# Moving edge loads, one head's row stores and the logit reads out of a prologue

## The chip, the cores and the metric

The kernel runs on one core of one Trainium2 chip. The metric is the device time of one execution in microseconds (us), as the median of several runs. Each profile shows one execution. Chips differ from one series of runs to the next: the median of the kernel before was 3262 to 3279 us in the five series of this study. So kernels are compared by their ratio to the kernel before in the same rounds. An execution can also fall in a slower state; all timed runs used here are of the fast one.

## The reference, cut to what matters

Two graph layers follow one another. Layer 0, the only one concerned, is attention over a given graph of 4096 nodes with four heads of 64 columns:

```python
h = relu(layernorm(x)) @ W            # (4096, 256), 4 heads
src, dst = h . a[:64], h . a[64:]     # logits per node and head
e = leaky_relu(src[:, :, None] + dst.T[None]);  e = where(adj > 0, e, -9e15)
x = x + layernorm(softmax(e) @ h)     # softmax and product per head
# layer 1: top-p attention with two steps over x, much longer, unchanged
```

The kernel never forms the softmax. For each source node it prepares rows of exponentials times `h`, splits them exactly into three bf16 parts, and multiplies them by 0/1 masks that say on which side of the leaky ReLU an edge falls.

## The kernel before

Layer 0 begins with a prologue over 32 blocks of 128 nodes; sixteen passes (four groups of 1024 targets by four heads) follow. One turn of the prologue, cut:

```python
for g in range(NB // 4):                      # NB = 32 blocks, in groups of four
    mv = rows.tile(..., name="mv4")           # 3 buffers
    ... moments of four blocks (VectorE), rs and nmr (GpSimd, 2 buffers each)
    for i in range(4):
        b = 4 * g + i
        nc.scalar.activation(hb, x4[:, i, :], AF.Relu, scale=rs, bias=nmr)
        ... 2 transposes of hb into pt
        nc.scalar.copy(hT, pt)
        ... 2 products of hT with wx into pm  (fp32, 264 columns)
        nc.vector.tensor_copy(sd_c[:, :, :, b], ...)             # logits
        ... uv = exp(logits) and rows times exp  (ScalarE, VectorE)
        parts = rows.tile([P, H, 2, W3 + 1], BF16, name="parts", bufs=6)
        set1 = nc.gpsimd.memset(parts[:, :, :, W3:], 1.0)
        nc.scalar.copy(parts[:, :, :, :W1], uv)                  # first part
        nc.vector.tensor_tensor(uv, uv, parts[...], ALU.subtract)
        if b % 3 == 2 and len(ax) < NB // 4:                     # 8 edge loads
            with tc.issue_after(set1.ins):
                ax.append(edges(0, len(ax)))                     # 1 MB each, from POOL
        ... second and third part
        nc.gpsimd.tensor_copy(ut0[b // QUARTER][:, b % QUARTER], parts[:, 0])
        nc.scalar.dma_start(uv_d[:, :, b]..., parts)             # row store, 4 heads
nc.sync.dma_start(s_d..., sT)                                    # logits to memory
```

The first pass starts with `g`, the mask input of targets: `g = relu(BIG * (src + dst))` from `sr`, the logits of 1024 targets spread over all partitions (read back from memory), then masks `m` against the edges `ax`, then products with the rows `ut`. Compute engines follow the written order in layer 0; the queue of SP (loads and stores of edges, rows and logits) does not and issues whatever is ready.

Of the kernel before, what the change touches and what calls it, by code (L numbers as in the profile page):

```python
# [11 lines left out]
F32 = mybir.dt.float32  # L12
F32R = mybir.dt.float32r
BF16 = mybir.dt.bfloat16
# [10 lines left out]
P = 128  # L25
# [12 lines left out]
G0 = 8  # L38
# [9 lines left out]
def gat_then_top_p_diffusion(  # L48
# [18 lines left out]
    nc = tc.nc  # L67
# [4 lines left out]
    NB = N // P  # L72
# [5 lines left out]
    small = ctx.enter_context(tc.tile_pool(name="small", bufs=4))  # L78
# [73 lines left out]
    with tc.tile_pool(name="l0", bufs=1) as l0, tc.tile_pool(name="l0a", bufs=9) as l0a, \  # L152
# [12 lines left out]
        ax = []  # L165
        QUARTER = NB // 4

        def quarter():
            return l0u.tile([P, QUARTER, 2, W3 + 1], BF16, name="ut")

        ut0 = [quarter() for q in range(4)]
        with tc.tile_pool(name="l0r", bufs=3) as rows, tc.tile_pool(name="l0w", bufs=1) as l0w, \
                tc.tile_pool(name="ps2", bufs=2, space=PSUM) as ps2:
            a_r = row_vector(a, "a_r", l0w)
            wx = l0w.tile([P, KC, D + 2 * H], F32, name="wx")
            nc.sync.dma_start(wx[:, :, :D], w.rearrange("(k p) m -> p k m", p=P))
            for k in range(KC):
                for i in range(2):
                    pr = l0w.tile([P, H, HD], F32, name="pr")
                    nc.vector.tensor_mul(pr, wx[:, k, :D].rearrange("p (h d) -> p h d", h=H),  # L180
                                         a_r[:, None, ts(i, HD)].to_broadcast([P, H, HD]))
                    nc.vector.reduce_sum(wx[:, k, ds(D + i * H, H)], pr, axis=AX.X)
            xs = [l0w.tile([P, 4, D], F32, name=f"x{g}") for g in range(NB // 4)]
            for g, x4 in enumerate(xs):
                nc.sync.dma_start(x4, x[ts(g, 4 * P), :].rearrange("(b p) d -> p b d", p=P))
            for g in range(NB // 4):
                x4 = xs[g]
                mv = rows.tile([P, 4, nc.vector.BN_AGGR_DIM], F32, name="mv4")
                for i in range(4):
                    moments_of(mv[:, i, :], x4[:, i, :])  # L190
                rs, nmr = steps(mv, 4, rows)
                for i in range(4):
                    b = 4 * g + i
                    hb = rows.tile([P, D], F32, name="hb")
                    nc.scalar.activation(hb, x4[:, i, :], AF.Relu, scale=rs[:, i:i + 1], bias=nmr[:, i:i + 1])
                    pt = ps2.tile([P, KC, P], F32, name="tp")
                    for k in range(KC):
                        nc.tensor.transpose(pt[:, k, :], hb[:, ts(k, P)], ident)
                    hT = rows.tile([P, KC, P], F32, name="hT")
                    nc.scalar.copy(hT, pt)  # L200
                    pm = ps2.tile([P, 512], F32, name="mm", bufs=3)
                    for k in range(KC):
                        nc.tensor.matmul(pm[:, :D + 2 * H], hT[:, k, :], wx[:, k, :], start=(k == 0), stop=(k == KC - 1))
                    nc.vector.tensor_copy(sd_c[:, :, :, b], pm[:, ds(D, 2 * H)].rearrange("p (t h) -> p t h", t=2))
                    uv = rows.tile([P, H, 2, W1], F32, name="uv")
                    for t, scale in enumerate((1.0, ALPHA)):
                        nc.scalar.activation(uv[:, :, t, HD:], pm[:, ds(D + H, H)][:, :, None], AF.Exp, scale=scale)
                    for t in range(2):
                        nc.vector.tensor_mul(uv[:, :, t, :HD], pm[:, :D].rearrange("p (h d) -> p h d", h=H),
                                             uv[:, :, t, HD:].to_broadcast([P, H, HD]))  # L210
                    parts = rows.tile([P, H, 2, W3 + 1], BF16, name="parts", bufs=6)
                    set1 = nc.gpsimd.memset(parts[:, :, :, W3:], 1.0)
                    nc.scalar.copy(parts[:, :, :, :W1], uv)
                    nc.vector.tensor_tensor(uv, uv, parts[:, :, :, :W1], ALU.subtract)
                    if b % 3 == 2 and len(ax) < NB // 4:
                        with tc.issue_after(set1.ins):
                            ax.append(edges(0, len(ax)))
                    nc.scalar.copy(parts[:, :, :, ds(W1, W1)], uv)
                    nc.vector.tensor_tensor(parts[:, :, :, ds(2 * W1, W1)], uv, parts[:, :, :, ds(W1, W1)], ALU.subtract)
                    nc.gpsimd.tensor_copy(ut0[b // QUARTER][:, b % QUARTER], parts[:, 0])  # L220
                    nc.scalar.dma_start(uv_d[:, :, b].rearrange("h p t w -> p h t w"), parts)
            pt = ps2.tile([P, KC, P], F32, name="tp")
            nc.tensor.transpose(pt[:, 0, :], s_c.rearrange("p h b -> p (h b)"), ident)
            sT = l0w.tile([P, P], F32, name="sT")
            nc.scalar.copy(sT, pt[:, 0, :])
            nc.sync.dma_start(s_d.rearrange("h (b i) -> (h b) i", b=NB), sT)
            w1_s, w2_s, w1_r = (l0w.tile(s, F32, name=x) for x, s in (
                ("w1_s", [P, KC, DA]), ("w2_s", [DA, DA]), ("w1_r", [DA, KC, P])))
            nc.scalar.dma_start(w1_s, w1_t.rearrange("(k p) m -> p k m", p=P))
            nc.scalar.dma_start(w2_s, w2_t)  # L230
            pt = ps2.tile([P, KC, P], F32, name="tp")
            for k in range(KC):
                nc.tensor.transpose(pt[:DA, k, :], w1_s[:, k, :], ident)
            nc.scalar.copy(w1_r, pt[:DA])
            for k in range(KC):
                pm = ps2.tile([P, 512], F32, name="mm", bufs=3)
                nc.tensor.matmul(pm[:, :DA], w1_r[:, k, :], w2_s, start=True, stop=True)
                nc.scalar.copy(wkq[:, k, DA:], pm[:, :DA])
            nc.vector.tensor_scalar(d_big, d_c, BIG, None, ALU.mult)

            for e, sign in zip(e_c, (1.0, -1.0)):
                nc.vector.tensor_scalar(e, s_c, sign * (1.0 - ALPHA), 0.0, ALU.mult, ALU.min)
                nc.scalar.activation(e, e, AF.Exp)

        with tc.tile_pool(name="l0m", bufs=3) as l0m, \
# [8 lines left out]
            def sources(k):  # L254

                ig, h = passes[k]
                sr = l0s.tile([P, G0 * P], F32, name="sr")
                nc.sync.dma_start(sr, s_d[h:h + 1, ts(ig, G0 * P)].to_broadcast([P, G0 * P]))
                shared[k] = SimpleNamespace(sr=sr, ut=[])

            def weighted(k, q):
                ut = quarter()
                nc.sync.dma_start(ut, uv_d[passes[k][1], :, ts(q, QUARTER)])
                shared[k].ut.append(ut)
# [10 lines left out]
            def masks(k, p, g):  # L275
                a = ax[p // 2][:, ds(2 * (p % 2), 2), :]
                m = [l0m.tile([P, 2, G0 * P], BF16, name=f"m{t}") for t in range(2)]
                nc.vector.tensor_tensor(m[0], g, a, ALU.min)  # L278
                nc.vector.tensor_tensor(m[1], a, m[0], ALU.subtract)  # L279
                return m  # L280

            def products(k, p, m):
# [75 lines left out]
            def sign_stage(n):  # L358
                if n < len(todo):
                    k, p = todo[n]  # L360
                    if n == 0:
                        sources(0)
                        shared[0].ut = ut0
                    gs[n] = signs(k, p)

            def mask_stage(n):
                if n < len(todo):
                    k, p = todo[n]
                    ig, h = passes[k]
                    if p % 4 == 0:  # L370

                        nq = k * 4 + p // 4 + 2
                        if 4 <= nq < 4 * len(passes):
                            if nq % 4 == 0:
                                sources(nq // 4)
                            weighted(nq // 4, nq % 4)
                    ms[n] = masks(k, p, gs.pop(n))
                    if h == 1 and p % 2:
                        nc.sync.dma_start(adj_d[ts(p // 2, 4), :, ts(ig, G0 * P)].rearrange("c p i -> p c i"), ax[p // 2])
                    if h == H - 1 and ig + 1 < NB // G0 and p % 2:  # L380
                        next_ax.append(edges(ig + 1, p // 2))
                    if h == H - 1 and p == PAIRS - 1:
                        ax[:] = next_ax
                        next_ax.clear()
# [724 lines left out]
```

## Time and profile before

| what | value |
|---|---|
| time | 3261.56 us, median of 3 (3259.44 to 3265.22); a fourth run came with the result |
| first row store issued | 31.46 us |
| last row store issued | 143.91 us, so 112.45 / 31 = 3.63 us a block |
| first `g` | 151.07 us |
| first pass closed (first `st<-acc` on ScalarE) | 199.16 us |
| layer 1's first big row operation (`big<-e,lowered`) | 1531.22 us |

### The profile page before, as it was taken

How to read it: one execution, taken by the hardware profiler on the slowest of the kernel's cores; microseconds unless marked ns; L12 is line 12 of the kernel's file. 1: busy time of each engine (PE TensorE's matmuls, PEld its weight loads, DVE VectorE, ACT ScalarE, POOL GpSimd, SP SyncE). 2: the span in 40 equal slices, each digit the busy share in tenths (PEclk: the TensorE clock that was granted, in tenths of full speed). 3: DMA queues.
4: the chain of work that ended last, by engine and by line, in shares of the span. 5: the costliest groups of instructions: out<-in, count | busy, mean ns of one | idle time of the engine just before them, and what ended most of it. 6: DMA issues, size and time to landing. Idle time of an engine off the chain costs nothing. (4 is left out here: it accounts for less than half of the span.)

```text
span 3276.4 us, 51761 instructions
## 1 busy us (share of the span) xinstructions
PE 2973.4 (91%) x19213; PEld 2417.6 (74%) x19213; DVE 2656.6 (81%) x5020; ACT 1952.7 (60%) x2903; POOL 1266.9 (39%) x1793
## 2 busy tenths in 40 slices
PE   4499899898989999986899999999879999999996
PEld 2299799797977888874677777777757777777785
DVE  6598899998976555546999999999469988888894
ACT  5588687786862110016577776775266777776742
POOL 3200100201000000003798998899015656656530
PEclk8699999999999999997899999999889999999998
DMA  9825639356225555520000000000100000000000
GB/s 260 228 83 144 204 113 255 117 142 206 73 85 181 165 177 164 161 89 1 10 19 15 16 20 15 15 18 17 62 13 10 25 20 25 22 22 25 20 27 13
DMA packets 198314, 268.48 MB, mean 82 GB/s; under 512 B 13728, under 2 KB 155552, under 8 KB 198048
## 3 DMA queue, kind: packets, MB, share of 16 engines
q1 hardware_dynamic: 152272, 207.99, 19.4%
q0 software_dynamic: 16896, 33.56, 5.7%
q10 hardware_dynamic: 28880, 23.48, 2.3%
q8 instruction: 155, 2.54, 0.3%
q14 instruction: 111, 0.91, 0.1%
HBM read 226.77 MB, written 71.76 MB: 91 GB/s over the span
## 5 line engine op out<-in xcount | busy, mean ns | idle before, releaser
L799 PE MATMUL acc<-X,eT 128*128 128x256 f32 x4160 | 978.4, 381 | 0.8 <-ACT eT L793 0.8
L799 PEld LDWEIGHTS acc<-X,eT 128*128 128x128 f32 x4160 | 762.6, 191 | 90.1 <-ACT eT L793 1.9
L291 PE MATMUL acc<-ut,m 128*128 128x195 bf16 (+1 forms) x8192 | 732.2, 249 | 82.3 <-DVE m L279 49.7
L291 PEld LDWEIGHTS <-m 128*128 128x128 bf16 x8192 | 703.4, 98 | 111.1 <-DVE m L279 66.9
L272 ACT ACTIVATE g<-sr,d_big 128x1024 bf16<-128x1024 f32 x512 | 550.6, 1178 | 50.2 <-DVE m L278 40.6
L618 ACT ACTIVATE void<-e,c 128x2048 int8<-128x2048 f32 x244 | 490.4, 2010 | 0.6
L611 ACT ACTIVATE e<-mm,nm 128x1024 f32<-128x1024 f32 x256 | 285.9, 1117 | 341.2 <-PE mm L488 338.1
L432 PE MATMUL racc<-hl,ar 128*128 128x512 f32 x2048 | 469.4, 391 | 16.8 <-issue 10.0
L432 PEld LDWEIGHTS racc<-hl,ar 128*128 128x128 f32 x2048 | 384.5, 188 | 101.5 <-issue 10.8
L791 PEld LDWEIGHTS tp<-ident,e 128*128 128x128 f32 x2080 | 246.8, 143 | 224.2 <-issue 126.6
L793 ACT COPY eT<-tp 128x512 f32<-128x512 f32 x520 | 303.4, 584 | 168.9 <-PE tp L791 168.1
L791 PE MATMUL tp<-ident,e 128*128 128x128 f32 x2080 | 327.9, 281 | 57.0 <-DVE e L728 42.8
L278 DVE TENSOR_TENSOR m<-g,ax 128x2048 bf16<-128x2048 bf16 x256 | 311.7, 1218 | 41.8 <-ACT g L272 38.8
L707 DVE MAX8 cand<-big 128x8 f32<-128x228 f32 (+1 forms) x1088 | 343.9, 395 | 0.1
L279 DVE TENSOR_TENSOR m<-ax,m 128x2048 bf16<-128x2048 bf16 x256 | 317.1, 1239 | 26.9 <-DVE m L278 1.4
L488 PE MATMUL mm<-kT,qT 64*128 64x512 f32 x1024 | 304.8, 678 | 33.5 <-ACT e L611 33.5
L428 DVE CAST ar<-at 128x1024 fp32r<-128x1024 bf16 x256 | 177.0, 692 | 169.8 <-PE racc L432 167.3
L694 DVE SCALAR_TENSOR_TENSOR big<-e,lowered 128x4096 f32<-128x4096 f32 x64 | 286.8, 4482 | 20.9 <-POOL lowered L639 20.9
L728 DVE SCALAR_TENSOR_TENSOR e<-e,found 128x4096 f32<-128x4096 f32 x64 | 286.7, 4480 | 0.0
L443 ACT ACTIVATE xf<-xf,rinv 128x256 f32<-128x256 f32 x64 | 32.7, 510 | 373.3 <-DVE xf L442 373.3
L648 POOL TENSOR_TENSOR sums<-sums 128x4 f32<-128x4 f32 (+1 forms) x64 | 106.4, 1662 | 378.8 <-ACT void L618 231.1
L488 PEld LDWEIGHTS mm<-kT,qT 64*128 64x128 f32 x1024 | 84.3, 196 | 130.6 <-issue 66.7
(245 smaller groups left out, 3269.4 us busy)
## 6 DMA issues: line engine op xcount, KB each, us to landing
at<-adj_d SPq DMA_DIRECT2D x256, 256.0 KB, 3.0
ut<-uv_d SPq DMA_DIRECT2D x60, 784.0 KB, 4.3
ax<-in_adj_t_dram POOLq DMA_DIRECT2D x32, 1024.0 KB, 13.6
adj_d<-ax SPq DMA_DIRECT2D x32, 1024.0 KB, 11.5
uv_d<-parts ACTq DMA_DIRECT2D x32, 392.0 KB, 8.2
xf<-xf_d SPq DMA_DIRECT2D x65, 128.0 KB, 2.0
sr<-s_d SPq DMA_DIRECT2D x16, 512.0 KB, 4.7
xf_d<-xf ACTq DMA_DIRECT2D x64, 128.0 KB, 2.4
```

The lines of the kernel that those rows point to most:

```text
L272: nc.scalar.activation(g[:, c, :], shared[k].sr, AF.Relu, scale=BIG, bias=d_big[:, h, j:j + 1])
L278: nc.vector.tensor_tensor(m[0], g, a, ALU.min)
L279: nc.vector.tensor_tensor(m[1], a, m[0], ALU.subtract)
L291: nc.tensor.matmul(shared[k].acc[i][:, t, :cols], m[t][:, c, ts(i, P)], shared[k].ut[j // QUARTER][:, j % QUARTER, t, :cols], start=(j == ...
L432: nc.tensor.matmul(acc[i].rearrange("p s d -> p (s d)"), ar[:, c, ts(i, P)], hl[hop][:, j].rearrange("p s d -> p (s d)"), start=(j == 0), ...
L488: nc.tensor.matmul(pm[:, h, :], q[ts(h, DA), :], kT[ts(h, DA), ts(c, 512)], start=True, stop=True)
L618: nc.scalar.activation(void, r.e[:, ts(h, N // 2)], (AF.Relu, AF.Sign)[i], bias=r.c1, scale=-1.0, accum_out=r.sums[:, h, 2 + i:3 + i])
L694: nc.vector.scalar_tensor_tensor(big, r.e, r.c3, r.e, ALU.is_le, ALU.mult, accum_out=r.L)
L707: nc.vector.max(cand[:, s, :], big[:, edges[s]:edges[s + 1]])
L791: nc.tensor.transpose(pt[:, i, :], r.e[:, ts(4 * g + i, P)], ident)
L793: nc.scalar.copy(eT, pt)
L799: nc.tensor.matmul(r.acc[:, 0, :], eT[:, i, :], cur[:, j, :], start=(j == 0), stop=(j == NB - 1))
```

## The change

Its intent is to spread transfers. The prologue has its transfer engines full and its compute engines waiting; the first pass is the reverse. Three of eight edge loads go behind the first mask, the rows of head 0 are stored by four large stores from `ut0` (on-chip copies that exist anyway) written in the code of the first pass (SP may issue them sooner), and the first targets' logits are spread by transposes rather than written and read back.

```diff
+        sr0 = l0.tile([P, G0 * P], F32, name="sr0")
...
-                    if b % 3 == 2 and len(ax) < NB // 4:
+                    if b % 6 == 5:
                         with tc.issue_after(set1.ins):
                             ax.append(edges(0, len(ax)))
...
-                    nc.scalar.dma_start(uv_d[:, :, b]..., parts)
+                    nc.scalar.dma_start(uv_d[1:, :, b]..., parts[:, 1:])
+                    if b % 4 == 3 and b < G0:
+                        pm = ps2.tile([P, 512], F32, name="mm", bufs=3)
+                        for i in range(4):
+                            nc.tensor.transpose(pm[:, ts(i, P)], s_c[:, 0, ds(b - 3 + i, 1)].to_broadcast([P, P]), ident)
+                        nc.scalar.copy(sr0[:, ds((b - 3) * P, 4 * P)], pm)
...  in the mask of the first pair:
+                if len(ax) < NB // 4:
+                    now = small.tile([P, 1], BF16, name="now", bufs=1)
+                    seen = nc.gpsimd.tensor_copy(now, m[0][:, 0, :1])
+                    with tc.issue_after(seen.ins):
+                        while len(ax) < NB // 4:
+                            ax.append(edges(0, len(ax)))
...
-                        sources(0)
-                        shared[0].ut = ut0
+                        shared[0] = SimpleNamespace(sr=sr0, ut=ut0)
...
+                    if k == 0 and p % 4 == 1:
+                        nc.sync.dma_start(uv_d[0, :, ts(p // 4, QUARTER)], ut0[p // 4])
```

More of the change, by code (lines that the diff above doesn't have):

```diff
@@ L220, in gat_then_top_p_diffusion @@
                     nc.gpsimd.tensor_copy(ut0[b // QUARTER][:, b % QUARTER], parts[:, 0])
-                    nc.scalar.dma_start(uv_d[:, :, b].rearrange("h p t w -> p h t w"), parts)
+                    nc.scalar.dma_start(uv_d[1:, :, b].rearrange("h p t w -> p h t w"), parts[:, 1:])
+                    if b % 4 == 3 and b < G0:
[3 more added lines that the diff above has]
+                        nc.scalar.copy(sr0[:, ds((b - 3) * P, 4 * P)], pm)
             pt = ps2.tile([P, KC, P], F32, name="tp")
```

## The prediction

> **What bounds the kernel now.** I read the mean busy times by stretch first, then the waits of ScalarE, then its order in time, then the DMA view, and last the order of instructions and waits in the two compiled programs. The change only touches layer 0's prologue (normalise 32 blocks, project, split into bf16 parts, store) and its first pass of masks and products, so the question is when that pass starts and whether it then runs as before.
>
> The stretches (columns: PE, PE weight load, DVE, ACT, POOL busy with counts, granted clock, DMA share, GB/s):
>
> ```profile
> 30.00:60.00 30.00, 17.12 (x52) 11.06 (x51) 22.15 (x61) 20.12 (x57) 13.41 (x28) 0.73 1.00 266
> 60.00:90.00 30.00, 18.59 (x64) 11.79 (x64) 21.65 (x50) 20.93 (x60) 11.75 (x26) 0.82 1.08 270
> 90.00:120.00 30.00, 10.78 (x33) 6.29 (x31) 13.88 (x31) 12.78 (x37) 7.60 (x19) 0.66 1.10 276
> 120.00:134.00 14.00, 5.08 (x16) 3.71 (x17) 3.83 (x10) 4.75 (x14) 2.75 (x8) 0.70 1.05 369
> 151.00:199.00 48.00, 43.46 (x487) 42.95 (x488) 41.34 (x35) 40.16 (x38) 0.00 (x0) 0.91 0.19 63
> ```
>
> From 30 to 134 us the 16 DMA engines are full (share 1.0 to 1.1) while no compute engine passes 75%; from 151 us on it is the reverse: PE 43.5 of 48 us, DMA 0.19. The prologue is bound by transfers and the first pass by PE, side by side in time. The waits of ScalarE in the prologue, and its own order, show how the transfers hold it:
>
> ```profile
> ACT parts L218 <- DMA adj_d<-ax: 18.0, 2, 10.4
> ACT uv L207 <- DVE sd_c L204: 14.0, 14, 2.8
> ACT g L272 <- DMA uv_d<-parts: 7.8, 1, 7.8
> ```
>
> ```profile
> 31.46 0.42 ACTq L221 DMA_DIRECT2D uv_d<-parts  x1
> 33.68 0.37 ACTq L221 DMA_DIRECT2D uv_d<-parts  x1
> 35.87 0.37 ACTq L221 DMA_DIRECT2D uv_d<-parts  x1
> ...
> 110.40 0.37 ACTq L221 DMA_DIRECT2D uv_d<-parts  x1
> 110.81 0.62 ACT L218 CAST parts<-uv 128x520 bf16<-128x520 f32 x1 [10.44 <-DMA adj_d<-ax]
> ...
> 143.91 0.37 ACTq L221 DMA_DIRECT2D uv_d<-parts  x1
> 151.07 1.15 ACT L272 ACTIVATE g<-sr,d_big 128x1024 bf16<-128x1024 f32 x1 [7.82 <-DMA uv_d<-parts]
> ```
>
> One store of rows per block: 2.2 us apart when free (31.46, 33.68, 35.87), but 112.45 us for 31 steps, 3.63 us each, in the whole. ScalarE's queue stands 10.4 us because the next row store shares a completion semaphore with an earlier store of edges and may not be issued before that has landed. POOL waits another 58 us in 17 pieces for row stores to free the parts buffers. The first mask input g starts at 151.07, 7.2 us after the last store's issue: it is written where parts lay, so it waits for that store to land.
>
> **What the Trainium skill says.** "DMA: Bandwidth & Descriptors", section "Issuing engines are not separate DMA queues": transfers issued by SP, ACT and POOL run on the same 16 engines and interleave. The trace agrees: row stores (ACT), edge loads (POOL) and edge stores (SP) together make the share of 1.0, and a row store takes 11.5 us to land in the second half of the prologue but 2.8 us at best. The same page's section "Rules for kernel authors" advises issuing transfers early, so that they overlap compute; here early issue is what fills the prologue, while the first pass has the engines at 0.19. "TensorE: Matmul & The Clock Gate", "Part 4: PE-mode transpose", gives about 275 ns for a 128x128 bf16 transpose inside a kernel; this trace has 273 ns (median) for its fp32 ones.
>
> **The change part by part.** Durations in DMA-engine time (share times stretch, divided by the transfers in it).
> (1) Edge loads. POOL's queue has a share of 5.7% of 3276 us for 32 loads: 5.84 us each. Before, nine are issued in the prologue (eight, and the ninth buffer is filled at once for the next targets); the compiled program shows five left and four behind the first mask: 4 x 5.84 = 23.4 us leave.
> (2) Edge stores. SP is not held to the written order: nine such stores are issued from 18 to 121 us, each as its load lands. SP's queue held 26.5%, 20.5% and 25.4% of the three 30 us stretches from 30 to 120, mostly these: 21.7 us for about 7.5 stores, 2.9 us each. With four loads go four stores: 11.6 us leave.
> (3) Row stores. The ACT queue has 34.5, 41.3, 28.1 and 38.3% of four 30 us stretches: 42.7 us for 32, 1.33 us each. A quarter (head 0) goes: 10.7 us leave. It comes back as four large stores from ut0; three of them are issued by SP inside the prologue, since they wait only for POOL's copies. The bytes alone would cost the same 2.7 us each; their runs are 6 KB instead of 784 bytes, so I estimate 2.2 us: 6.6 us come back.
> (4) Spread logits. The 512 KB reads sr<-s_d (issued at 141.2 and 142.0, 3.5 to 6.4 us to land) no longer precede g. But they land by about 147 to 148, while g waits until 151 for the last row store; and in the new program g still waits for the store s_d<-sT. So this alone gains nothing. It costs 8 transposes x 0.27 = 2.2 us on PE, half idle there, and two copies of 128x512, like the 0.58 us rows of the page: 1.2 us on ScalarE.
> Sum on the DMA engines: -23.4 - 11.6 - 10.7 + 6.6 = -39 us. The old budget was about 147 us (52.6 loads, 26 edge stores, 42.7 row stores, some 15 for x and weights, some 10 for reads at the end), which fits g at 151; the new one is 108.
>
> Not all of the 39 arrives, since two other limits come up. Compute: 31.5 + 31 x 2.4 us (2.2 seen free, a little for groups and the spread) + 1.5 for the copies = 107, plus about 5 to land: 112. And the ring of semaphores: in the new program the last row store (block 31) waits for the fifth edge store to land, and that of block 25 for the fourth. The fifth load is issued when the row store of block 23 has landed: 31.5 + 1.5 + 23 x 2.4 = 88, plus 4 behind the fourth's stall, landed near 93; load 11 us (10.5 to 15.4 seen), edge store 6.5 (5.3 to 17.6 seen): 111; the last row store then lands at 116 to 117. I take 117 for g, so 34 us earlier than 151.
>
> The first pass then carries the load that left: 4 x 5.84 + 4 x 2.9 + 2.2 and the next head's reads, some 50 us of engine time. It needs the sixth edge tile at its pair 10, which DVE reached 28.5 us after g (179.55 - 151.07), the seventh at 34, the eighth at 39.4. Issued from about 4.5 us after g, one behind the other, they land near 12, 20 and 28. So I count no stall. The pass for the fourth head already runs so: 291 to 337 us with DMA share 0.97, in the same 46 us as the pass before it with 0.25. All behind it is in order and bound by compute, so the start's gain should reach the end: 3261.6 - 34 = 3228.
>
> **The rivals.** (a) The semaphore ring takes the place of what is removed: a fifth load of 15 us and an edge store of 10, as seen at full share, put g at 125 to 128, and the time is 3236 to 3239. For it: 18 us of just this wait in the kernel before. Against it: fewer transfers in flight. (b) Compute becomes the bound: g at 106 to 112, time 3216 to 3223; for it the steps of 2.2 us wherever nothing is late. (c) The late edges stall the first pass, since three loads in one burst meet stores and reads: a median of 11.9 us to landing but a maximum of 25.1 in the first 420 us. If the eighth took 45 us the pass would lose 5 to 10 us: 3233 to 3238. (d) The transfers were hidden anyway and nothing moves: against it stands that every engine idles in the prologue, and ScalarE waits on transfers by name.
>
> **Range and chances.** The DMA sum alone bounds the gain at 39, perfect compute at 45, the bad ring or late edges leave about 20. So 3228, from 3216 to 3242. Two per cent is 65 us, and more than half of the 120 us between the first row store and g would have to go: 1% for faster. For slower by 65 us all of the first pass would have to wait twice over: 1%.
>
> **What would show it.** g's first start near 117 instead of 151 (between 108 and 128). In the stretch from 30 us to g a DMA share under 1.0 in its first third and five edge loads, not nine; in the 45 us after g a share of 0.8 to 1.1 with PE still near 43 of 48 us. ScalarE's last row store just after an edge store's landing shows the ring; DVE's mask at pairs 10, 12 or 14 waiting on a DMA of edges would show rival (c). It is wrong if g comes later than 130, if the first pass grows by over 5 us, or if later passes, which should keep 46 us, change length.

## The result, and the profile after

The changed kernel took 3246.16 us (median of 4, 3240.59 to 3252.81) against 3262.1 us (median of 4, 3259.44 to 3265.22). The ratio is 0.9952, 95% interval 0.9931 to 0.9973: really faster, and less so than the predicted 3228 us. A ratio here is the mean time of one kernel's fast runs over that of the other's of the same rounds, so not quite the ratio of the medians quoted.

The same stretches as in the prediction, in the profile of the changed kernel (columns: PE, PE weight load, DVE, ACT, POOL busy with counts, granted clock, DMA share, GB/s):

```profile
30.00:60.00 30.00, 16.13 (x51) 9.50 (x49) 20.91 (x54) 18.60 (x50) 11.21 (x21) 0.76 0.58 152
60.00:90.00 30.00, 16.48 (x51) 10.68 (x52) 20.78 (x51) 19.85 (x55) 14.23 (x33) 0.73 0.76 220
90.00:120.00 30.00, 18.90 (x62) 11.91 (x62) 20.76 (x49) 21.04 (x59) 10.16 (x22) 0.78 0.96 259
138.70:186.70 48.00, 43.51 (x484) 42.95 (x485) 41.48 (x34) 40.27 (x38) 4.15 (x5) 0.90 0.86 227
```

The transfers did leave: the share is 0.58 in the first third where it was 1.00, and 0.86 in the first pass where it was 0.19. But the compute engines did not fill the freed time: VectorE is busy 20.9 of 30 us, where it was 22.2. The first pass keeps its PE time (43.51 of 48 us, before 43.46). ScalarE's order in time, and the waits of the prologue (line waiting, what ended the wait, total us, times, longest):

```profile
30.56 0.38 ACTq L222 DMA_DIRECT2D uv_d<-parts  x1
33.93 0.37 ACTq L222 DMA_DIRECT2D uv_d<-parts  x1
37.21 0.37 ACTq L222 DMA_DIRECT2D uv_d<-parts  x1
...
125.98 0.37 ACTq L222 DMA_DIRECT2D uv_d<-parts  x1
129.55 0.37 ACTq L222 DMA_DIRECT2D uv_d<-parts  x1
138.72 1.15 ACT L279 ACTIVATE g<-sr,d_big 128x1024 bf16<-128x1024 f32 x1 [10.04 <-DMA uv_d<-ut]
```

```profile
POOL parts L213 <- DMA uv_d<-parts: 31.5, 12, 7.7
POOL ut L221 <- DVE parts L220: 30.2, 18, 5.6
ACT parts L219 <- DVE uv L215: 20.7, 24, 7.5
DVE sd_c L205 <- PE mm L204: 18.4, 20, 1.7
ACT uv L208 <- DVE sd_c L205: 9.2, 11, 1.5
DVE mv L140 <- POOL nmr L133: 7.4, 1, 7.4
```

No line of ScalarE waits for `adj_d<-ax` any more (18.0 us before). Rows are (129.55 - 30.56) / 31 = 3.19 us apart, not 3.63, and `g` starts 9.2 us after the last one instead of 7.2. So it starts 12.35 us earlier than before. The first pass closes at 187.15 us, 12.0 earlier (48.4 us after `g`, before 48.1), and layer 1's first big operation comes at 1519.04, 12.2 earlier: the shift of the start is carried through layer 0 unchanged, and within the noise it is the whole gain. (The two profiled executions lie 25.5 us apart in all; the other 13 us arise in layer 1, which the change doesn't touch, and the profiled run of the kernel before was itself 16 us over its median. The ratio, 15.7 us, is the figure to hold against the shift. In two later series it was 0.9958 and 0.9961, or 12.7 to 13.8 us. Layer 1, which has the same code in all runs, took 1728 to 1749 us in the profiles with exact products, so single whole times hide shifts of some us, and the marks in layer 0 are the finer measure.)

One wait stands out. This is the changed kernel from 52 to 63 us, cut to the instructions that matter (start, duration, engine and line, with the idle time before and what ended it in brackets):

```profile
49.88 0.33 SPq L391 DMA_DIRECT2D uv_d<-ut  x1
52.26 0.37 ACTq L222 DMA_DIRECT2D uv_d<-parts  x1
...
60.06 0.13 POOL L213 MEMSET parts<- 128x8 bf16 x1 [6.92 <-DMA uv_d<-parts]
60.28 0.23 POOL L131 TENSOR_SCALAR rs<-mv 128x4 f32<-128x4 f32 x1
60.60 0.23 POOL L133 TENSOR_SCALAR nmr<-mv 128x4 f32<-128x4 f32 x1
60.80 1.05 POOL L132 TENSOR_TENSOR rs<-rs,mhalf 128x4 f32<-128x4 f32 x1
60.86 0.38 DVE L140 BATCH_NORM_AGGREGATE mv<-st 128x2 f32<-128x6 f32 x4 [7.42 <-POOL nmr L133]
...
61.91 0.37 ACTq L222 DMA_DIRECT2D uv_d<-parts  x1
62.47 0.63 ACT L219 CAST parts<-uv 128x520 bf16<-128x520 f32 x1 [7.46 <-DVE uv L215]
```

Read it backwards. No row leaves between 52.26 and 61.91. ScalarE waits for VectorE, VectorE stands before the moments of a later group, because their buffer `mv4` has yet to be read by POOL's `nmr`; and POOL stands in front of a memset of eight columns, which needs a `parts` buffer whose row store has not landed. At that moment an edge load (issued 47.8) and the new large store of head 0 (49.88) are in flight. A tiny instruction on a waiting engine, in written order, has become the coupling.

### The profile page after: what moved, and what is told of

The parts are those of the page before. It is cut to its first block, busy times and chain, and to the rows that moved or that the text cites. A ratio compares the mean times of both kernels' runs of the same rounds, so it can differ in the third digit from the quotient of the medians.

```text
span 3250.9 us, 51785 instructions
## 1 busy us (share of the span) xinstructions
PE 2971.6 (91%) x19221; PEld 2417.0 (74%) x19221; DVE 2654.3 (82%) x5020; ACT 1950.0 (60%) x2905; POOL 1128.3 (35%) x1794
## 5 line engine op out<-in xcount | busy, mean ns | idle before, releaser
L447 PE MATMUL racc<-hl,ar 128*128 128x512 f32 x2048 | 471.7, 392 | 16.6 <-issue 11.2
L458 ACT ACTIVATE xf<-xf,rinv 128x256 f32<-128x256 f32 x64 | 32.6, 510 | 374.1 <-DVE xf L457 371.7
## 6 DMA issues: line engine op xcount, KB each, us to landing
ax<-in_adj_t_dram POOLq DMA_DIRECT2D x32, 1024.0 KB, 13.8
xf<-xf_d SPq DMA_DIRECT2D x65, 128.0 KB, 2.0
xf_d<-xf ACTq DMA_DIRECT2D x64, 128.0 KB, 2.5
```

What stands on the lines that cost most here:

```text
L447: nc.tensor.matmul(acc[i].rearrange("p s d -> p (s d)"), ar[:, c, ts(i, P)], hl[hop][:, j].rearrange("p s d -> p (s d)"), start=(j == 0), ...
```

## The experiments

Four suspects were left after the traces: transfers still in flight (T below where the texts use a letter), the buffers through which a late row store stops POOL and VectorE, the time of PE's fp32 products, and the tail between the last row and `g`. All kernels gave correct results. In the table "pace" is the mean distance of the row stores and the last column is the ratio to the kernel before in the same rounds.

| run | what | pace us | `g` at us | ratio [95%] |
|---|---|---|---|---|
| kernel before | | 3.63 | 151.1 | 1 |
| changed kernel | three profiles | 3.19, 3.24, 3.31 | 138.7, 141.0, 139.6 | 0.9952, 0.9958, 0.9961 |
| e1 | one edge load in the prologue | 3.10 | 133.4 | 0.9987 [0.9963, 1.0012] |
| e2 | nine `parts` buffers | 3.06 | 131.1 | 0.9926 [0.9906, 0.9945] |
| e3 | SP in written order | 3.20 | 142.5 | 1.0038 [1.0019, 1.0058] |
| e4 | eight buffers for moments | 3.04 | 130.0 | 0.9941 [0.9920, 0.9961] |
| e6 | filler products | 3.03 | 128.0 | 0.9956 [0.9937, 0.9975] |
| e7 | rounded products | 3.07 | 128.6 | 1.0107 [1.0091, 1.0124] |
| e8 | later reads held back | 3.21 | 135.6 | 0.9945 [0.9928, 0.9961] |
| e9 | edge part alone | 3.02 | 133.6 | 0.9933 [0.9920, 0.9947] |
| e10 | head and logit part alone | 3.56 | 150.6 | 0.9989 [0.9975, 1.0002] |
| e11 | one load, rounded products, buffers | 2.64 | 116.1 | one look |
| e12 | both buffers, reads held back | 2.98 | 126.5 | 0.9925 [0.9912, 0.9939] |
| e13 | rounded products, buffers | 2.67 | 117.9 | one look |
| e14 | one load, buffers | 2.98 | 131.0 | one look |
| e15 | edge part, logits, buffers, reads held | 3.12 | 130.7 | 0.9935 [0.9921, 0.9948] |

### First series: one suspect at a time

**e1, edges.** Are the transfers that are left what holds the prologue?

```diff
-                    if b % 6 == 5:
+                    if b == 5:
```

> The changed kernel with one edge load (not five) left in the prologue and seven behind the first mask. What holds the row stores at 3.19 us per block? Theory T (transfers: a row store that shares the engines with an edge transfer lands late, and POOL and then everything waits for a parts buffer): without edge transfers the spacing falls to 2.4 us and g starts near 111 us. Theory E (engines: order of the instructions and PE's low granted clock): spacing stays near 3, g starts at 130 or later. In both the first pass must now wait for its edges: seven loads of 5.8 to 7 us against 5.5 us of products per edge tile, so the pass grows by 5 to 15 us. Time T: about 3230; E: about 3248.

Measured: the share of the transfer engines fell to 0.36 between 30 and 110 us, and yet rows left 3.10 us apart. The 9.6 us stall of the changed kernel was gone (2.7), but steps of 5.5 to 6.5 us stayed elsewhere. So transfers alone are not what holds the changed prologue. In return the first pass stalled: seven late edge tiles stopped VectorE's masks for 23.1 us, the pass took 67.9 us from `g` to its close instead of 48.4, and the gain was gone (the expectation had allowed 5 to 15 us for this; it was 19.5). Of the three splits tried, one, five or eight loads before the mask, five is the best.

**e2, parts buffers.** Nine instead of six (the room came from placing another tile in a scratch tile that is no longer used).

```diff
-                    parts = rows.tile([P, H, 2, W3 + 1], BF16, name="parts", bufs=6)
+                    parts = rows.tile([P, H, 2, W3 + 1], BF16, name="parts", bufs=9)
```

> The changed kernel with nine parts buffers in place of six (the sT tile takes the place of an old scratch tile to make room). Theory T: POOL's 31.5 us of waits for row stores fall under 12, spacing falls to about 2.7, g starts 8 to 15 us earlier (124 to 131). Theory E: POOL's waits fall too, but the spacing stays at 3.1 to 3.2 and g moves by less than 4 us.

Measured: pace 3.06, `g` at 131.1, ratio 0.9926. It helps (`g` 7.6 us earlier), but POOL still waits 26.6 us in 14 pieces for row stores where theory T said under 12; neither theory's numbers hold.

**e3, SP in written order.** This keeps the stores of edges from being issued as soon as their data is there. (The run's edit also drops the `issue_after` of the late loads; they were issued 4.75 us after `g` as before.)

```diff
-            every = {ET.DVE, ET.PE, ET.Activation, ET.Pool}
+            every = {ET.DVE, ET.PE, ET.Activation, ET.Pool, ET.SP}
```

> The changed kernel with SP held to the written order in layer 0, so that all edge stores leave the prologue for the second pass, and the reads for the next heads come when written. Theory T: 14.5 us of edge stores leave a prologue that is full in its last third; g starts 8 to 15 us earlier, time near 3234. Theory E: g moves by less than 4 us, time within 3242 to 3250.

Measured: pace 3.20, as without. The edge stores left the prologue and the rows went no faster. Later passes grew: the fifth took 66.9 us, in the changed kernel 64.0, the sixth 52.7 against 49.0, and so in each group of targets. In the fifth and sixth VectorE waits 6.0 us for POOL's work on `xb`, the block of `x` read back, against 0.7 in the changed kernel. So the kernel became slower than before, outside both expectations. The free order of SP is worth keeping.

**e4, buffers for a group's moments.** With eight buffers of `mv4`, `rs4` and `nmr4`, VectorE need not wait for POOL as it did at 60.86.

```diff
-            rs, nmr = (pool.tile([P, n], F32, name=x, bufs=2) for x in (f"rs{n}", f"nmr{n}"))
+            rs, nmr = (pool.tile([P, n], F32, name=x, bufs=8 if n == 4 else 2) for x in (f"rs{n}", f"nmr{n}"))
-                mv = rows.tile([P, 4, nc.vector.BN_AGGR_DIM], F32, name="mv4")
+                mv = rows.tile([P, 4, nc.vector.BN_AGGR_DIM], F32, name="mv4", bufs=8)
```

> The changed kernel with eight buffers for the moments of four blocks and for their scales (three and two before), so that DVE's moments no longer wait for POOL to read an older group. In the changed kernel's order DVE stood 7.4 us at 61 us in one such wait, behind a POOL that waited for a row store. Theory T: this link only passes on a wait for a transfer; the wait moves to another buffer and g moves by less than 5 us. Theory E (order of engines): g starts 6 to 12 us earlier.

Measured: pace 3.04, ratio 0.9941. The waits of POOL for row stores grew to 42.7 us, but they stopped VectorE no longer, and `g` came 8.8 us earlier, in the range of theory E. So the stall was the coupling, as read from the trace; 0.15 to 0.27 us a block hang on it, by which of the three profiles of the changed kernel one compares with.

Three different cures, each ending at 3.04 to 3.10: this looks like a second limit close behind the first.

### Second series: PE's products and the tail

**e5, control.** The changed kernel again.

> The changed kernel once more, as the control of this batch: 3240 to 3253 us, g starts at 135 to 141 us if the prologue is the same in every execution; how far it differs from 138.7 says how far single profiles may be trusted.

Measured: pace 3.24, `g` at 141.0, ratio 0.9958 [0.9941, 0.9974].

In e1 the granted clock was 0.50 from 55 to 70 us, and a block's products then make a ring with ScalarE and VectorE, which the trace of e1 shows step by step:

```profile
58.38 0.37 ACT L201 COPY hT<-tp 128x256 f32<-128x256 f32 x1
58.80 2.13 PE L204 MATMUL mm<-wx,hT 128*128 128x264 f32 x4 [0.46 <-ACT hT L201]
60.72 0.63 PE L199 MATMUL tp<-ident,hb 128*128 128x128 f32 x2
60.97 0.17 DVE L205 COPY sd_c<-mm 128x8 f32<-128x8 f32 x1 [1.57 <-PE mm L204]
61.17 0.24 ACT L208 ACTIVATE uv<-mm 128x4 f32<-128x4 f32 x2 [1.06 <-DVE sd_c L205]
61.39 0.37 ACT L201 COPY hT<-tp 128x256 f32<-128x256 f32 x1
61.81 2.13 PE L204 MATMUL mm<-wx,hT 128*128 128x264 f32 x4 [0.46 <-ACT hT L201]
```

The products of one block start at 58.80 and of the next at 61.81: 3.01 us. ScalarE copies `hT` only after the exponentials of the block before, and these wait for its products. At full clock the four matmul records take 1.16 us instead of 2.13.

**e6, filler products.** Two 128x512 bf16 products into a spare tile after the transposes and after the products, in the hope that a busy PE keeps its clock up.

```diff
+            def spin(n):
+                if n:
+                    pb = ps2.tile([P, 512], F32, name="spin", bufs=1)
+                    for _ in range(n):
+                        nc.tensor.matmul(pb, busy[:, :P], busy, start=True, stop=True)
```

> The changed kernel with four matmuls of 128x512 bf16 without use per block of the prologue (two behind the transposes, two behind the products), to keep PE busy. Theory E2: with fewer waits for transfers the prologue is a ring PE, ScalarE, PE, in which a block takes 2.0 to 2.2 us at a granted clock of 1.0 and 3.0 at 0.5, and the clock stood at 0.5 for about half of the prologue. If the extra work lifts the clock to 1.0 from 30 us on, the spacing of the row stores falls to 2.3 to 2.7 us and g starts at 113 to 124. If the clock stays at 0.5, the spacing grows to 3.5 or more. Theory E1 (the order of the instructions alone, whatever the clock): the clock may rise, but the spacing stays at 3.0 to 3.3.

Measured: the clock stood at 1.00 from 30 to 60 us but at 0.79 and 0.73 in the next two stretches of 30 us, so it was lifted for only half the prologue. Pace 3.03, `g` at 128.0. Layer 0 ended 12.5 us earlier than in the control (1507.31 against 1519.77), yet the ratio is the control's; the trace doesn't say why. Inconclusive: the clock was not lifted throughout, the 9.6 us stall happened to be missing too (see e9), and with the fillers PE is busy 28.4 of the 30 us from 30 to 60.

**e7, rounded products.** Operands in the rounded 32-bit format (fp32r), so that two records replace four.

```diff
+            wr = l0w.tile([P, KC, D + 2 * H], F32R, name="wr")
+            nc.vector.tensor_copy(wr, wx)
-                    hT = rows.tile([P, KC, P], F32, name="hT")
+                    hT = rows.tile([P, KC, P], F32R, name="hT")
-                        nc.tensor.matmul(pm[:, :D + 2 * H], hT[:, k, :], wx[:, k, :], ...)
+                        nc.tensor.matmul(pm[:, :D + 2 * H], hT[:, k, :], wr[:, k, :], ...)
```

> The changed kernel with the products of the prologue in fp32r in place of fp32 (rounded inputs; the result may miss the reference's tolerance, on purpose). It makes PE's part of the ring shorter at either clock. Theory E2: spacing falls to 2.2 to 2.6, g at 110 to 122. Theory E1, or theory T: spacing 2.9 or more, g at 130 or later.

Measured: still correct, pace 3.07, `g` at 128.6, but the whole is 1% slower than before. VectorE's wait for the products fell from 20.6 us to 5.9. One step of 10.5 us remained, in which POOL waited for row stores up to 11.2 us. The loss arises in layer 1, which ran 4224 instead of 4160 products on line `acc<-X,eT`; perhaps the rounded rows change data on which its path depends. That was not tested, so the whole times of e7, e11 and e13 say nothing about the prologue. The record of the granted clock says 1.00 from 30 to 110 us here. It is wrong, as the transposes of `hb` show, which are fp32 in all runs: e6 from 32 to 60 us, recorded at 1.00, and this run (count, then ns min/median/max):

```profile
L208 PE MATMUL tp<-ident,hb x12: 270/272/273, 36.3 to 56.6; 128*128 128x128 f32 x12
L201 PE MATMUL tp<-ident,hb x44: 415/421/476, 35.6 to 109.5; 128*128 128x128 f32 x44
```

In e1, recorded at 0.50 from 55 to 70 us, the median is 421 ns too. So this prologue ran at half clock, and so did those of e11 and e13 (421 ns each).

**e8, the tail.** The reads of logits for the next heads and the fourth large store are held behind first masks by touching their tiles with a small POOL instruction there.

```diff
+                if k < 3:
+                    nc.gpsimd.memset(sr[:, :1], 0.0)
+                    if k == 0 and p == 13:
+                        nc.gpsimd.tensor_copy(ut0[3][:, 0, 0, :1], ut0[3][:, 0, 0, :1])
```

> The changed kernel with the two reads of spread logits for heads 1 and 2 and the last store of head 0's rows held behind the first mask (one-element writes of POOL make them wait). In the changed kernel the last row store took 8.9 us to land beside them and g waited for it. Expected under all theories of the spacing: the spacing stays near 3.2, g follows the last row store by 4 to 5.5 us in place of 9.2, so g starts about 4 us earlier and the time falls by about 4 us, not clear of the noise.

Measured: `g` follows the last row by 3.45 us, in the control by 8.3; it starts at 135.6, 5.4 us earlier than in the control. The ratio is 0.9945; by means the control took 3258.36 us and this one 3258.01, so the time does not resolve these 5 us; the trace does.

### Third series: the parts of the change, and several cures at once

**e9, the edge part alone.**

```diff
 (the changed kernel with the stores, logits and reads of the kernel before)
-                    nc.scalar.dma_start(uv_d[1:, :, b]..., parts[:, 1:])
+                    nc.scalar.dma_start(uv_d[:, :, b]..., parts)
-                        shared[0] = SimpleNamespace(sr=sr0, ut=ut0)
+                        sources(0)
+                        shared[0].ut = ut0
```

> One part of the change alone: five edge loads in the prologue and three behind the first mask, but all row stores and the logits' reads as in the kernel before. By the recorded sum this part is 35 of the 39 us of transfers, so nearly the whole gain. Theory of several limits (row store landing before a memset, half the granted clock, one fixed order, each near 3.0 to 3.2 us a block): rows 3.2 to 3.4 us apart (3.63 before, 3.2 to 3.24 with the whole change), g at 139 to 145, ratio to the kernel before 0.995 to 0.998. Rival, that the row stores' bytes set the pace and the edge part does little: rows 3.5 us apart, ratio 0.999.

Measured: pace 3.02, `g` at 133.6, ratio 0.9933. The edge part alone has all of the gain, and by its one trace rather more than the whole change. The trace at the place where the changed kernel stalled:

```profile
52.04 0.13 POOL L212 MEMSET parts<- 128x8 bf16 x1
52.26 0.24 POOL L131 TENSOR_SCALAR rs<-mv 128x4 f32<-128x4 f32 x1
52.57 0.23 POOL L133 TENSOR_SCALAR nmr<-mv 128x4 f32<-128x4 f32 x1
```

No wait: the row store had landed, and no large store was in flight. e1 had the large store and no edge load at this point and did not stall either. So it seems to take both, and POOL's order as well: e6 has both and POOL stands 7.0 us for a row store, but only after its `nmr`, and no row is held up for 9.6 us. The three profiles of the changed kernel, e3, e7 and e8 all have a step of 9.4 to 10.5 us here.

**e10, the other part alone.**

```diff
-                    if b % 6 == 5:
+                    if b % 3 == 2 and len(ax) < NB // 4:
```

> The other part alone: the first head's rows are stored later and its logits spread by transposes, but all eight edge loads stay in the prologue (one every three blocks). By the recorded sum only 4 us of transfers leave, so g comes at 145 to 149 and the ratio is about 0.999. If the reads of logits and rows at the end were what counted after all, g would move by 6 us or more and the ratio be under 0.9975.

Measured: pace 3.56, `g` at 150.6 (its own range said 145 to 149), ratio 0.9989 with an interval that includes 1. The large stores and the spread logits bring nothing by themselves, as the prediction said of the logits.

**e11, three cures at once.** One load as in e1, rounded products as in e7, eight buffers of `parts` (nine in e2) and of the moments as in e4.

> Three suspected limits lifted at once in the changed kernel: one edge load in the prologue, products in the rounded format that ran at the full granted clock, and eight buffers for parts and for a group's moments. Each alone left 3.04 to 3.10 us between rows. Theory that limits of nearly the same size overlap: 2.2 to 2.6 us between rows, g at 108 to 115. Rival, that one further limit common to all (the order of the instructions on ScalarE and VectorE) sets 3.0 us: spacing stays at 2.9 to 3.1. The late edges will hold the first pass as they did with one load, and layer 1 will be long as with the rounded products, so its whole time says nothing.

Measured: pace 2.64, `g` at 116.1. The theory of overlapping limits holds in its main point, and the rival of a fixed 3.0 us falls; but the pace is just above the 2.2 to 2.6 expected. The premise of a full clock was wrong: the record says 0.50 here, and by its transposes e7 had no more.

```profile
30.00:110.00 80.00, 38.27 (x115) 23.15 (x114) 68.75 (x175) 62.65 (x176) 36.26 (x71) 0.50 0.50 168
```

**e12, what could be used.** Nine buffers of `parts`, five of the moments, the tail as in e8, exact products.

> Wider buffers in the changed kernel (nine for parts, five for a group's moments) together with the reads and the fourth large store held behind the first mask: meant to beat both kernels. Alone they gave spacings of 3.06 and 3.04 and took 5.4 us from the tail. Theory of overlapping limits: spacing about 2.9 to 3.0, tail 3.5 to 4, g at 125 to 127, about 13 us before the changed kernel's, ratio to the kernel before 0.991 to 0.992. If buffers and tail only share one and the same gain: g near 130, ratio 0.993 to 0.994.

Measured: pace 2.98, tail 2.7 us, `g` at 126.5, ratio 0.9925. The step to 126.5 came as expected, the ratio just short of it.

### Fourth series: which of the last limits, and a control

**e13, rounded products and buffers, all five loads in place.**

> The changed kernel with rounded products (full granted clock in the prologue) and eight buffers for parts and for a group's moments, but with all five edge loads in the prologue. If the clock is what the last 0.35 us a block hang on (2.98 with buffers alone, 2.64 with buffers, clock and one load): rows 2.65 to 2.75 us apart, g at 117 to 122. If the edge transfers are: 2.9 to 3.0, g at 125 to 128. The whole time says nothing, since layer 1 is longer with rounded products.

Measured: pace 2.67, `g` at 117.9, first pass closed at 166.64, layer 1's first big operation at 1499.10. The stretch from 30 to 110 us, of e13 and then of e12:

```profile
30.00:110.00 80.00, 37.72 (x114) 22.90 (x113) 69.55 (x175) 61.60 (x175) 35.25 (x75) 0.51 0.92 254
```

```profile
30.00:110.00 80.00, 48.07 (x153) 29.92 (x154) 60.63 (x148) 56.85 (x155) 30.56 (x64) 0.74 0.82 217
```

VectorE goes from 60.63 to 69.55 busy us of 80, with the transfer engines fuller than before (0.92). What changed is PE: 37.72 us of work instead of 48.07. It is not a higher clock, since the record says 0.51 against 0.74 and the transposes agree (see e7); the expectation had the right side with the wrong reason. The rounded products are short even at half clock: from their start to VectorE's copy of the logits, where nothing else was in the way, 0.84 to 0.85 us passed in e13, e11 and e7 alike, against 2.16 in the changed kernel at half clock.

**e14, one load and buffers, exact products.**

> The changed kernel with one edge load in the prologue and wider buffers, but with the exact products that run at half the granted clock for part of the time. If the clock is the last limit: rows 2.9 to 3.0 us apart as with the buffers alone and g at 125 to 128. If the edge transfers are: 2.65 to 2.75 and g at 116 to 120. The first pass stalls for late edges as it did with one load.

Measured: pace 2.98, exactly as e12 with five loads; `g` at 131.0 (it lacks e12's held reads). The edge transfers make next to nothing of the last 0.3 us; e11 and e13, which differ in the edge loads alone, say the same (2.64 and 2.67). These runs suggest the order: buffers first, PE's product step second, transfers no more. (The buffers are not quite alike: e12 has nine of `parts`, the others eight; e12 and e14 have five of the moments, e11 and e13 eight.)

**e15, a version to beat both.** The edge part and the spread logits without the large stores, with the buffers and held reads of e12.

```diff
 (e12 with the row stores of the kernel before)
-                    nc.scalar.dma_start(uv_d[1:, :, b]..., parts[:, 1:])
+                    nc.scalar.dma_start(uv_d[:, :, b]..., parts)
-                    if k == 0 and p % 4 == 1:
-                        nc.sync.dma_start(uv_d[0, :, ts(p // 4, QUARTER)], ut0[p // 4])
```

> The edge part of the change and the spread logits, without the large stores of the first head, with nine buffers for parts, five for a group's moments and the next heads' logits held behind the first mask. If the large stores cost more than they saved: rows 2.85 to 2.98 us apart, g at 122 to 126, ratio to the kernel before 0.9905 to 0.992, at least as good as the wider buffers with the large stores (0.9925). If they saved transfers as I recorded: rows 3.0 to 3.1, g at 128 to 131, ratio 0.993 to 0.994.

**e16, control.** The changed kernel in the same rounds.

> The changed kernel as it is, a control of the same rounds: rows 3.2 us apart, g at 138 to 141, ratio 0.995 to 0.996 as in its two batches before. If it shows 0.993 here, the difference to the edge part alone was only that between batches.

Measured: e15 took 3246.84 us (3246.29 to 3248.56), the control 3255.49 (3250.81 to 3259.30), the kernel before 3268.45; ratios 0.9935 [0.9921, 0.9948] and 0.9961 [0.9947, 0.9975]. The runs of e15 and of the control do not overlap: e15 is 0.26% faster than the changed kernel by the means (3247.16 / 3255.65). Its pace is 3.12 against e12's 2.98, as the expectation's second case had it (rows 3.0 to 3.1, `g` at 128 to 131). So with wide buffers the large stores may save a little, as I had recorded of their bytes; but the changed kernel alone varies from 3.19 to 3.31, and layer 0 ended at 1509.78 in e15 and 1510.97 in e12, so it isn't shown. Which of e12 and e15 is the faster kernel stays open, as they ran in different series; both beat the kernel before by 0.6 to 0.8%.

## Why the prediction was wrong

The prediction was too hopeful: 3228 us with a range from 3216 to 3242, against 3246. `g` came at 138.7, beyond its own line of 130 for being wrong. Point by point:

**The sum of transfers was right.** It said 39 us of engine time would leave (about 147 to 108). Share times time up to `g`: before 0.98 x 30 + 0.99 x 121 = 149 us; after 0.85 x 30 + 0.80 x 108.7 = 112 us. That is 37 us less. The step from this sum to `g` is what failed.

**"No stall" and "carried to the end" were right.** The first pass took 48.4 us from `g` to its close (48.1 before) at a share of 0.86, the next three kept 46.1 to 46.4 us, and the shift of 12 us arrived whole in layer 1. Rival (c) did not happen with three late loads, but did with seven (e1).

**Rival (a), the ring of semaphores, was wrong as the limit.** In the changed kernel no row store waited for an edge store, though e10, which keeps all loads, still had 13.6 us of such waits. The 117 us of the prediction were the ring's number; without it the compute term should have bounded at 112.

**The step that failed is the compute term, "31.5 + 31 x 2.4 us (2.2 seen free, a little for groups and the spread) + 1.5 for the copies = 107, plus about 5 to land: 112".** Its terms measured: start 30.56 instead of 31.5 (-0.9), 31 x 3.19 instead of 31 x 2.4 (+24.6), no extra 1.5, and 9.2 us to `g` instead of 5 (+4.2). With the 112.4 of the sum before rounding these give 138.7, but for rounding.

The 24.6 us have three pieces, which e11 to e14 tell apart (estimates from single paces; those of the changed kernel alone differ by 0.12 us a block, 3.7 us, so good to no more than that):

- With buffers and short products the pace was still 2.67, or 0.27 us a block above 2.4: 8 us. Here VectorE is busy 69.55 of 80 us in which 30 row stores left, 2.32 us a block. At 2.4 us it would have had to be 97% busy. This could have been read blind: in the stretches that the prediction itself shows, VectorE's busy times from 30 to 134 us sum to 61.5 us, in which 28 rows left, 2.2 us a block. The free steps of 2.2 us that I took as the pace are the first four of the kernel before, and in them VectorE is already busy 8.41 of 8.94 us:

  ```profile
  31.46:40.40 8.94, 4.13 (x16) 2.52 (x16) 8.41 (x19) 6.63 (x21) 3.35 (x6) 0.99 0.98 339
  ```

  So 2.2 us is nearly VectorE's own time for a block, a floor and not a pace. These steps had what later ones lacked: a recorded clock of 0.99 (0.59 from 40 to 60 us), and six `parts` buffers set by 18.60 us; the seventh memset, at 37.45, waits for a row store.
- Exact products at half clock: 2.98 to 2.67, or 0.31 us a block: 10 us. They tie PE, VectorE and ScalarE in the ring of 3.0 us that e1's trace shows. I had named PE only as "half idle there", and the 273 ns that I gave for its transposes is the median over two speeds, 272 and 421 ns.
- Buffers through which a late row store stops POOL and then VectorE: 3.19 to 2.98, or 0.21 us a block: 6.5 us (0.26 to 0.33 with the two other profiles of the changed kernel). I had seen POOL's 58 us of waits and left them out of the compute term; they are a coupling that shows even at a share of 0.58.

Lifting one piece brings little, because the next is waiting at about 3.05; this fits e1, e2, e4, e6 and e7 looking alike. With two lifted, e13 put `g` at 117.9 and layer 0's end 32.1 us earlier than before (1531.22 to 1499.10), close to the predicted 117 and 34. So the claimed start is reachable, by cures that the prediction did not name; the change alone does not reach it. What each remaining wait of e12 costs was not followed instruction by instruction.

**The tail.** "About 5 to land" became 9.2. I expected three of the four large stores inside the prologue and overlooked that SP, which is free in its order, would issue the fourth (130.14) and the next heads' logits (128.96) right beside the last row store. The row store landed 8.9 us after its issue and the fourth large store 8.5 us after its own, both at about 138.5, and then `g` started. e8, which holds them back, has 3.45 us. The control e16 has 5.1 us, the predicted 5: there the reads (134.71) and the large store (135.60) were issued after the last row store (134.50). So the 9.2 us is one order of SP's among several, not a fixed cost.

**What the parts are worth.** Edges carry the gain (0.9933 alone). The large stores and the logits bring none alone that is clear of noise (0.9989), and the 4 us that I credited to the stores are less than the one stall that came with them. That e9 beats the whole change rests on one trace of it against three of the changed kernel (133.6 against 138.7 to 141.0 for `g`, 1513.6 against 1518.0 to 1519.8 for layer 0's end) and is only suggested by the times, which come from different series.

## What to carry to other kernels

When a bound is lifted, the fastest step in the trace is not the new pace: divide every engine's busy time by the units of work it covers, and ask what the fast steps had that the later ones lacked (here a full clock and free buffers). Where several limits lie within a few per cent of each other, curing one at a time shows almost nothing for each; run two or three cures together before dropping a theory. A small instruction in written order on a waiting engine can pass a late transfer on to the busy engines, and one more buffer for what stands behind it may be worth more than fewer bytes.

## What the Trainium skill lacked or had wrong

- "TensorE: Matmul & The Clock Gate", "Part 1: The HAM clock gate (the "warmup" mystery)", says that the clock is gated to half after an idle window of about 3.4 us and that recorded events have been unreliable. The window was not tested here; two speeds are seen (fp32 transposes of 272 and 421 ns). The second point decided a reading here: e7's record shows 1.00 for the whole of 30 to 110 us, with PE busy 32.6 of 80 us, while e13 and e11 show 0.51 and 0.50 at 37.7 and 38.3 us. From the products' start to the dependent copy it is 0.84 to 0.85 us in all three, and the transposes take 421 ns in all three, so the records differ and the speed does not. The page advises a cross-check against the total of throttled time; what it lacks is a check for one stretch: the duration of an instruction that is the same in all runs, or the interval between a product and the instruction that waits for it (for exact products 1.1 to 1.2 us against 2.16 to 2.17).
- "FP8 and Floating Point Precision", "TensorE Precision Notes", gives four passes for true fp32. The traces show two records for each exact 264-column product (four for a block's two) and one for each rounded one; how records and passes go together is not shown, and the page has no time for the rounded format. Here a block's pair took 0.81 us rounded and 2.13 us exact, both at half clock.
- "DMA: Bandwidth & Descriptors", "Rules for kernel authors", advises early issue. It lacks the case in which early transfers crowd later, urgent ones: three loads of 1 MB issued later gave a ratio of 0.9933 (e9). It lacks the other side too: seven issued later cost 23.1 us of waiting for masks (e1).
- No page that I used says how far a late transfer reaches through small buffers: six `parts` buffers and three of `mv4` turned one late landing into 7.4 us of waiting on VectorE; widening either gave 0.13 to 0.27 us a block.
